# Layer 2 running sums: a written order on TensorE, head-sized state products, and the second norm on ScalarE

## The chip, the cores and the metric

The kernel runs on one core of a Trainium2 chip. The metric is device microseconds of one launch, taken as the median of several runs. Besides the timed runs there is one execution recorded by the hardware profiler; all durations of single instructions come from it. Engines are named as the profile names them: PE is TensorE's matrix array, PEld its weight load, DVE is VectorE, ACT is ScalarE, POOL is GpSimd, SP is SyncE.

## The reference, cut to what matters

The network has four layers on 4096 tokens of 256 channels (32 tiles of 128 tokens). The change lies in layer 2, a gated linear attention with 8 heads of 32 channels followed by a mixture of experts. Its attention is

```
q, k, v = linear(x)                        # per head 32 channels
k = l2_normalize(k); v = l2_normalize(v)
Z = v (x) k * kv_norm_scale                # one 32x32 matrix per token and head
gates = square(relu(Z . wg + wg_b)) + EPS
Z_scan = cumsum(gates * Z); g_scan = cumsum(gates)
w = exp(sim - running max) / (running sum + EPS)
ctxt = q . (Z_scan / (g_scan + EPS)) * (1 + silu(w))
out = linear(ctxt, wo_w, wo_b)
```

and after `x + out`, the expert layer normalises its input (mean and variance over the 256 channels), adds the normalised rows to the residual, and routes each token to the best two of eight experts by the normalised row:

```
n = layernorm(x); logits = n @ router; top-2; x = x + n + (experts' outputs)
```

The sum `Z_scan` over tokens is what the function `attn2_sum` computes, in chunks: inside a tile of 128 tokens by a 128x128 table of scores with a triangular mask, from earlier tiles by a 32x32 state per head that is added up tile by tile.

## The kernel before, in words

`run` goes through the layers one after another. Layer 2 is `attn2` (line 1169). It projects all tokens to q, k and v, normalises and gates them, then works out in `attn2_fac` one factor per token and head, and then calls `attn2_sum` (line 1423), the stage that the change rewrites. After it come a short `tile_table` and the experts of layer 2, which start by loading the rows that the last router step scattered to memory.

`attn2_sum` has 16 turns of its loop, one for each pair `u` of token tiles. In a pair:

- POOL multiplies q by the factor (line 1434) and adds the output bias to the residual `t` (1435).
- PE turns q to channels (four transposes, 1439, into the PSUM bank with the tag "o"); ACT copies the result to `qT` (1441).
- PE makes the scores, 16 products of 32 rows by 128 columns (1449), in two PSUM tiles `s`; DVE multiplies each with the triangle to `sm` (1452, 1024 columns, two a pair).
- For each of the two tiles, PE adds into the context bank `c` what earlier tiles give: `before[:, m, :]`, a 128x128 matrix for four heads at once, in which all blocks but the four on the diagonal have to be zero (1462). Then it makes the tile's own state, a 128x128 product of v and k (through the helper at line 146, tile `st_ps`); DVE adds it to the running `state` (1471) and multiplies the sum with a block mask `ones_bd` to make the next `before` (1473). Then PE adds to `c` what the tile itself gives, eight products with 32 output rows (1477).
- ACT scales `c` to `cT` (1484, two a pair); PE multiplies with the output weights (line 146, tile `o_ps`, the same bank "o"); DVE adds this to `t` (1488).

Matrix products are float32; in the profile each stands as two rows, a transpose as one.

In the same loop runs the router step `route` (line 1731) of the four tiles that were finished two pairs before. It is a generator: `next(steps)` runs it to its next `yield`. Its parts are the norm (DVE at line 213, then POOL adds the normalised rows to `t`, line 1741); two sets of four transposes (1747) with a copy on ACT and one on DVE; the router product with 8 columns (through 146, `f_r_ps<-w_r`) and the choice of the best two, some twenty DVE instructions of 0.2 us and an exponential on ACT; a product for the positions, and eight scattering transfers on POOL (1784). The square root of the norm (204) and the exponential (1724) each need their own function table in ACT, so both load one, eight times each.

All these PSUM tiles but `s` have one buffer: "o" (shared by the transposes of q and the output product), "c", "state" and the router's "r". The order of the work on each engine is set by a scheduler that merges the instructions by its own estimate of times; each engine then works its list strictly in order. Nothing in the stage is written by hand. The projection before it does write the order on PE by hand, with `manual_schedule(engines={PE})`: PE's instructions then stand as the program writes them, and the other engines' are still placed by the scheduler.

Of the kernel before, what the change touches and what calls it, by code (L numbers as in the profile page):

```python
# [10 lines left out]
F32 = mybir.dt.float32  # L11
# [77 lines left out]
class Net:  # L89
# [102 lines left out]
    def layer_norm(self, pool, x, out, eps, on_act=False):  # L192
# [16 lines left out]
        for i in range(n):  # L209
            if on_act:  # L210
                nc.scalar.activation(to(i), x[:, i, :], AF.Identity, bias=shift[:, i : i + 1], scale=r[:, i : i + 1])
            else:
                nc.vector.tensor_scalar(to(i), x[:, i, :], mv[:, i, 0:1], r[:, i : i + 1], ALU.subtract, ALU.mult)

# [962 lines left out]
    def attn2(self, t, S):  # L1177

        nc, tc = self.nc, self.tc
        with tc.tile_pool(name="a2", bufs=1) as pool:  # L1180
# [8 lines left out]
            ones_bd = pool.tile([P, 2, P], F32, tag="ones_bd", name="ones_bd")  # L1189
            self.kv_blocks(pool, None, wg_bd)  # L1190
            nc.gpsimd.memset(ones_bd, 0.0)
            for h in range(4):
                hp = slice(h * D, (h + 1) * D)
                nc.gpsimd.memset(ones_bd[hp, :, hp], 1.0)
# [28 lines left out]
            with (  # L1223
# [11 lines left out]
                self.attn2_sum(t, A, ked, ones_bd, wp, ps, route)  # L1235
# [187 lines left out]
    def attn2_sum(self, t, A, ked, ones_bd, wp, ps, route):  # L1423
# [3 lines left out]
        state = wp.tile([P, 2, P], F32, tag="state", name="a2_state", bufs=1)  # L1427
        before = None
        steps = None
        for u in range(NT // 2):  # L1430
            two = slice(2 * u, 2 * u + 2)
            q, k = A["qk"][:, two, 0:C], A["qk"][:, two, C:]
            qh = q.rearrange("p t (h d) -> p t h d", d=D)
            nc.gpsimd.tensor_tensor(qh, qh, bc(A["fac"][:, :, u, :], 3, D), ALU.mult)
            nc.gpsimd.tensor_tensor(t[:, two, :], t[:, two, :], bc(self.row("wo_b"), 1, 2), ALU.add)
            p = ps.tile([P, 2, 2, P], F32, tag="o", name="a2_qT_ps")
            for m in range(2):
                for j in range(2):
                    nc.tensor.transpose(p[:, m, j, :], q[:, j, m * P : (m + 1) * P], self.ident)
            qT = wp.tile([P, 2, 2, P], F32, tag="qT", name="a2_qT")  # L1440
            nc.scalar.copy(qT, p)
            sms = []
            for pair in range(2):
                s = ps.tile([P, 2, 2, 2, P], F32, tag="s", name="a2_s", bufs=2)
                for m in range(2):
                    for j in range(2):
                        for i in range(2):
                            hp = slice((2 * pair + i) * D, (2 * pair + i + 1) * D)
                            nc.tensor.matmul(s[:, i, m, j, :], A["vT"][hp, m, (2 * u + j) * P : (2 * u + j + 1) * P], qT[hp, m, j, :],
# [3 lines left out]
                sms.append(sm.rearrange("p i (m j) n -> p i m j n", m=2))  # L1453
            if steps:
                next(steps, None)
            c = ps.tile([P, 2, 2, P], F32, tag="c", name="a2_c_ps")
            first = True
            for j in range(2):
                ti = 2 * u + j
                for m in range(2):  # L1460
                    if before is not None:
                        nc.tensor.matmul(c[:, m, j, :], before[:, m, :], qT[:, m, j, :], start=first, stop=False)
                        first = False
                if ti < NT - 1:
                    sp = ps.tile([P, 2, P], F32, tag="state", name="a2_st_ps")
                    for m in range(2):
                        self.mm(sp[:, m, :], [(A["v"][:, ti, m * P : (m + 1) * P], k[:, j, m * P : (m + 1) * P])])
                    if ti == 0:
                        nc.vector.tensor_copy(state, sp)
                    else:  # L1470
                        nc.vector.tensor_add(state, state, sp)
                    nxt = wp.tile([P, 2, P], F32, tag="before", name="a2_before", bufs=3)
                    nc.vector.tensor_mul(nxt, state, ones_bd)
                for m in range(2):
                    for h in range(4):
                        hp = slice(h * D, (h + 1) * D)
                        nc.tensor.matmul(c[hp, m, j, :], k[:, j, m * P + h * D : m * P + (h + 1) * D], sms[h // 2][:, h % 2, m, j, :],
                                         start=(before is None and m == 0), stop=(j == 1 and m == 1))
                if before is None:
                    first = False  # L1480
# [985 lines left out]
```

## Time and profile before

| | us |
|---|---|
| median of 3 runs (lowest, highest) | 3781.54 (3780.37, 3785.58) |
| the profiled execution | 3747.99 |
| its span | 3746.2 |
| PE busy in the span | 3401.1 |
| first product of the stage to the end of its last output product | 1795.5 to 2014.2 |
| of this, pairs 0 to 3 (first transposes of q to the end of the scores of pair 4) | 1796.8 to 1852.9 |
| of this, the rest of pair 4 to pair 15 | 1852.9 to 2014.2 |
| end of the last output product to the experts' first load | 2014.2 to 2045.1 |

The profiled execution is some 34 us shorter than the timed runs. Times of day are microseconds from the start of the span. A busy PE is not a PE at its peak: its clock is granted in full or in part, and the profile gives the granted share for any stretch.

### The profile page before, as it was taken

How to read it: one execution, taken by the hardware profiler on the slowest of the kernel's cores; microseconds unless marked ns; L12 is line 12 of the kernel's file. 1: busy time of each engine (PE TensorE's matmuls, PEld its weight loads, DVE VectorE, ACT ScalarE, POOL GpSimd, SP SyncE). 2: the span in 40 equal slices, each digit the busy share in tenths (PEclk: the TensorE clock that was granted, in tenths of full speed). 3: DMA queues.
4: the chain of work that ended last, by engine and by line, in shares of the span. 5: the costliest groups of instructions: out<-in, count | busy, mean ns of one | idle time of the engine just before them, and what ended most of it. 6: DMA issues, size and time to landing. Idle time of an engine off the chain costs nothing. (4 is left out here: it accounts for less than half of the span.)

```text
span 3746.2 us, 59679 instructions
## 1 busy us (share of the span) xinstructions
PE 3401.1 (91%) x22332; PEld 2387.8 (64%) x22332; DVE 2211.1 (59%) x5433; ACT 1360.4 (36%) x2783; POOL 1433.0 (38%) x1416
## 2 busy tenths in 40 slices
PE   6989999999997788887787977999999996999997
PEld 4433333333343688855565755888888885888886
DVE  6756656666565477778665557777777775111111
ACT  5544343443432566433121334222222222323231
POOL 1038888888884455534343433000000001111110
PEclk9999999999998899999786989999999997999999
DMA  1004414401013322200012865223223322555554
GB/s 57 3 28 115 132 42 119 121 24 41 21 41 105 104 68 77 73 19 1 12 44 100 255 219 225 90 96 95 91 91 102 96 91 96 203 191 190 195 186 182
DMA packets 160975, 378.27 MB, mean 101 GB/s; under 512 B 17377, under 2 KB 75490, under 8 KB 151458
## 3 DMA queue, kind: packets, MB, share of 16 engines
q1 hardware_dynamic: 136450, 318.96, 26.2%
q0 software_dynamic: 13056, 35.93, 2.5%
q10 hardware_dynamic: 11168, 19.42, 1.5%
q8 instruction: 182, 2.98, 0.3%
q14 instruction: 119, 0.97, 0.1%
HBM read 273.96 MB, written 100.29 MB: 100 GB/s over the span
## 5 line engine op out<-in xcount | busy, mean ns | idle before, releaser
L583 POOL TENSOR_TENSOR l_sm<-l_sc,mask 128x512 f32<-128x512 f32 (+3 forms) x624 | 770.0, 1271 | 118.6 <-ACT l_sc L573 116.2
L577 DVE TENSOR_TENSOR l_sm<-l_s,mask 128x256 f32<-128x256 f32 (+3 forms) x1248 | 492.6, 448 | 299.9 <-PE l_s L567 290.3
L573 ACT COPY l_sc<-l_s 128x384 f32<-128x384 f32 (+3 forms) x896 | 367.8, 461 | 556.9 <-PE l_s L567 540.9
L567 PE MATMUL l_s<-l_q,l_k 32*128 32x384 f32 (+2 forms) x3584 | 423.6, 513 | 7.4 <-ACT l_sc L573 4.1
L1784 POOL DMA_INDIRECT xs<-f_n,f_to x64 | 62.8, 981 | 788.0 <-DVE a_qt L2096 576.5
L146 PE MATMUL f_h_ps<-f_xT,f_w 128*128 128x256 f32 x1440 | 346.5, 389 | 13.9 <-ACT f_h L1898 5.8
L1925 POOL DMA_INDIRECT ys<-f_y,f_at x144 | 138.8, 964 | 575.4 <-ACT f_y L1924 527.3
L146 PE MATMUL f_y_ps<-f_w,f_h 128*128 128x256 f32 x1440 | 328.1, 379 | 0.0
L146 PEld LDWEIGHTS f_h_ps<-f_xT,f_w 128*128 128x128 f32 x1440 | 266.2, 192 | 83.1 <-ACT f_h L1898 31.6
L567 PEld LDWEIGHTS l_s<-l_q,l_k 32*128 32x128 f32 x3584 | 164.9, 183 | 240.5 <-issue 123.2
L146 PEld LDWEIGHTS f_y_ps<-f_w,f_h 128*128 128x128 f32 x1440 | 268.2, 190 | 33.6
L2144 ACT ACTIVATE a_e<-a_e 128x512 f32<-128x512 f32 x256 | 156.9, 629 | 241.3 <-DVE a_e L2117 240.4
L952 DVE TENSOR_TENSOR l_pr<-l_vk,l_w_ps 128x1280 f32<-128x1280 f32 x128 | 186.6, 1482 | 55.1 <-PE l_acc_ps L956 37.7
L1898 ACT ACTIVATE f_h<-f_h_ps,f_w 128x256 f32<-128x256 f32 x360 | 163.6, 468 | 134.3 <-PE f_h_ps L146 134.2
L956 PE MATMUL l_acc_ps<-ident,l_pr 128*128 128x128 f32 x1600 | 196.9, 277 | 9.4 <-POOL l_pr L947 9.2
L956 PEld LDWEIGHTS l_acc_ps<-ident,l_pr 128*128 128x128 f32 x1600 | 183.5, 143 | 15.7 <-POOL l_pr L947 10.9
L1924 ACT ACTIVATE f_y<-f_y,f_wgt 128x256 f32<-128x256 f32 x144 | 65.3, 500 | 328.6 <-DVE f_y L1922 295.8
L610 PE MATMUL l_a_ps<-l_sm,l_v 128*32 128x512 f32 (+3 forms) x1408 | 178.2, 528 | 2.6 <-POOL l_sm L583 2.5
L610 PE MATMUL l_b_ps<-l_sm,l_v 128*32 128x256 f32 (+2 forms) x2176 | 171.5, 376 | 0.5 <-POOL l_sm L583 0.5
L2128 PE MATMUL a_sa_ps<-a_q,a_kt 128*128 128x256 f32 x512 | 155.2, 385 | 17.9 <-DMA a_kt<-a_kd 9.3
L2132 ACT COPY a_u<-a_sa_ps 128x256 f32<-128x256 f32 x128 | 47.6, 372 | 328.3 <-PE a_sa_ps L2128 328.3
L1922 DVE TENSOR_TENSOR f_y<-f_y_ps,f_w 128x512 f32<-128x512 f32 x72 | 49.8, 691 | 196.7 <-PE f_y_ps L146 190.4
(500 smaller groups left out, 6301.1 us busy)
## 6 DMA issues: line engine op xcount, KB each, us to landing
a_kt<-a_kd SPq DMA_DIRECT2D x128, 512.0 KB
f_w<-in_f_w SPq DMA_DIRECT2D x36, 1152.0 KB
f_w<-in_f_w SPq DMA_DIRECT2D x36, 1028.0 KB
xs<-zero SPq DMA_DIRECT2D x8, 4160.0 KB
l_vk<-vt SPq DMA_DIRECT2D x180, 128.0 KB
f_x<-xs SPq DMA_DIRECT2D x72, 260.0 KB
f_w<-in_f_w SPq DMA_DIRECT2D x36, 384.0 KB
l_rcp<-l_recd SPq DMA_DIRECT2D x48, 256.0 KB
```

The costliest lines, as they stand in the source:

```text
L146: self.nc.tensor.matmul(out, lhsT, rhs, start=(i == 0), stop=(i == len(pairs) - 1))
L567: nc.tensor.matmul(s[pair, j], k[hp, key * P : (key + 1) * P], qs[hp], start=True, stop=True)
L573: nc.scalar.copy(sc[:, j], s[1, j])
L577: nc.vector.tensor_tensor(sms[0][:, j, at : at + t * wide].rearrange("p (t n) -> p t n", n=wide), part[:, which, :], mask, ALU.mult)
L583: nc.gpsimd.tensor_tensor(sms[1][:, :, at : at + t * wide].rearrange("p j (t n) -> p j t n", n=wide), part[:, :, which, :], bc(mask, 1, 2) ...
L610: nc.tensor.matmul(out, v[:, key, hp], sms[pair][:, j, base + lo * wide : base + hi * wide], start=not seen[nm], stop=(left[nm] == 0 and h ...
L952: nc.vector.tensor_tensor(pr, vk, bc(held["w"][:, j, dy], 3, D), ALU.mult)
L956: nc.tensor.matmul(acc[:, m, j, :], pf[:, dx, m * P : (m + 1) * P], self.ident, is_transpose=True, start=(j == 0 and dy == 0 and dx == 0 a ...
L1898: nc.scalar.activation(h[:, m, :], q, AF.Gelu, bias=w1[:, 2 * hidden + m : 2 * hidden + m + 1])
L1925: nc.gpsimd.indirect_dma_start(out=self.ys_parts[(i % 4) * NI + k], in_=y[:, k, :], in_offset=None, out_offset=bass.IndirectOffsetOnAxis(a ...
L2128: mm = lambda out, i, right: nc.tensor.matmul(out, A[i], right, start=True, stop=True)
L2144: nc.scalar.activation(e[:, i : i + 3 : 2], e[:, i : i + 3 : 2], AF.Exp, scale=1.0 / 16.0)
```

## The change

- PE's order in the stage is written out. A turn of the loop issues: the transposes of q of the next pair (`turn`), the states of this pair (`states`), the output product of the pair before (`out`), one step of the router, the context of this pair (`context`), the scores of the next pair (`scores`), and another step of the router.
- What earlier tiles give is applied head by head: four 32x32 products for each half of the channels (`earlier`) in place of one 128x128 product. The off-diagonal blocks of the state are thus never read, and the mask `ones_bd` with its multiplication goes. `before[ti+1]` is itself the running sum (a DVE add from `before[ti]` and PSUM).
- The states of both tiles of a pair are made together, in one PSUM bank.
- `earlier` for both tiles stands in front of `within`, what the tiles themselves give.
- The router's norm of layer 2 is made on ACT (`on_act`, line 211: scale and shift), and so is the sum of the residual and the normalised rows: `t*(r+1)+shift`, four ACT instructions in place of one on POOL. DVE makes the shift and `r+1`, two small instructions.

```diff
+        return r, (shift if on_act else None)
...
-            ones_bd = pool.tile([P, 2, P], F32, tag="ones_bd", name="ones_bd")
...
-            nc.gpsimd.memset(ones_bd, 0.0)
-            for h in range(4):
-                hp = slice(h * D, (h + 1) * D)
-                nc.gpsimd.memset(ones_bd[hp, :, hp], 1.0)
...
-                self.attn2_sum(t, A, ked, ones_bd, wp, ps, route)
+                self.attn2_sum(t, A, ked, wp, ps, route)
...
-    def attn2_sum(self, t, A, ked, ones_bd, wp, ps, route):
+    def attn2_sum(self, t, A, ked, wp, ps, route):
         nc, w = self.nc, self.w
         tri = self.triangle(wp)
...
+        qTs, sms, before, cTs = {}, {}, {}, {}
+        two = lambda u: slice(2 * u, 2 * u + 2)
+        keys = lambda ti: A["qk"][:, ti, C:]
+        def scale(u):
+            qh = A["qk"][:, two(u), 0:C].rearrange("p t (h d) -> p t h d", d=D)
             nc.gpsimd.tensor_tensor(qh, qh, bc(A["fac"][:, :, u, :], 3, D), ALU.mult)
...
+            nc.gpsimd.tensor_tensor(t[:, two(u), :], t[:, two(u), :], bc(self.row("wo_b"), 1, 2), ALU.add)
+        def turn(u):
             p = ps.tile([P, 2, 2, P], F32, tag="o", name="a2_qT_ps")
             for m in range(2):
                 for j in range(2):
...
+                    nc.tensor.transpose(p[:, m, j, :], A["qk"][:, 2 * u + j, m * P : (m + 1) * P], self.ident)
+            qTs[u] = wp.tile([P, 2, 2, P], F32, tag="qT", name="a2_qT")
+            nc.scalar.copy(qTs[u], p)
+        def scores(u):
+            sms[u] = []
             for pair in range(2):
                 s = ps.tile([P, 2, 2, 2, P], F32, tag="s", name="a2_s", bufs=2)
                 for m in range(2):
                     for j in range(2):
                         for i in range(2):
                             hp = slice((2 * pair + i) * D, (2 * pair + i + 1) * D)
...
+                            nc.tensor.matmul(s[:, i, m, j, :], A["vT"][hp, m, (2 * u + j) * P : (2 * u + j + 1) * P], qTs[u][hp, m, j, :],
                                              start=True, stop=True)
                 sm = wp.tile([P, 2, 4, P], F32, tag="sm", name="a2_sm", bufs=3)
                 nc.vector.tensor_tensor(sm, s.rearrange("p i m j n -> p i (m j) n"), bc(bc(tri, 1, 4), 1, 2), ALU.mult)
...
+                sms[u].append(sm.rearrange("p i (m j) n -> p i m j n", m=2))
+        def states(u):
+            sp = ps.tile([P, 2, 2, P], F32, tag="state", name="a2_st_ps")
+            for j in range(2):
+                for m in range(2):
+                    self.mm(sp[:, j, m, :], [(A["v"][:, 2 * u + j, m * P : (m + 1) * P], keys(2 * u + j)[:, m * P : (m + 1) * P])])
             for j in range(2):
                 ti = 2 * u + j
...
+                before[ti + 1] = wp.tile([P, 2, P], F32, tag="before", name="a2_before", bufs=4)
+                if ti == 0:
+                    nc.vector.tensor_copy(before[1], sp[:, 0])
+                elif ti < NT - 1:
+                    nc.vector.tensor_add(before[ti + 1], before[ti], sp[:, j])
+        def context(u):
+            c = ps.tile([P, 2, 2, P], F32, tag="c", name="a2_c_ps")
+            def earlier(j, first):
                 for m in range(2):
                     for h in range(4):
                         hp = slice(h * D, (h + 1) * D)
...
+                        nc.tensor.matmul(c[hp, m, j, :], before[2 * u + j][hp, m, hp], qTs[u][hp, m, j, :], start=(first and m == 0), stop=False)
+            def within(j, first):
+                for m in range(2):
+                    for h in range(4):
+                        hp = slice(h * D, (h + 1) * D)
+                        nc.tensor.matmul(c[hp, m, j, :], keys(2 * u + j)[:, m * P + h * D : m * P + (h + 1) * D], sms[u][h // 2][:, h % 2, m, j, :],
+                                         start=(first and m == 0), stop=(j == 1 and m == 1))
+            if u == 0:
+                within(0, True)
+                earlier(1, False)
+            else:
+                earlier(0, True)
+                earlier(1, False)
+                within(0, False)
+            within(1, False)
+            cTs[u] = wp.tile([P, 2, 2, P], F32, tag="cT", name="a2_cT")
             for m in range(2):
...
+                nc.scalar.activation(cTs[u][:, m], c[:, m], AF.Identity, scale=ked[:, m, 0:1])
+        def out(u):
             o = ps.tile([P, 2, C], F32, tag="o", name="a2_o_ps")
             for j in range(2):
...
+                self.mm(o[:, j, :], [(cTs[u][:, kt, j, :], w["w_o2"][:, kt, :]) for kt in range(2)])
+            nc.vector.tensor_add(t[:, two(u), :], t[:, two(u), :], o)
+        U = NT // 2
+        steps = []
+        def step():
+            for s in list(steps):
+                if next(s, self) is self:
+                    steps.remove(s)
+        with self.tc.manual_schedule(engines={mybir.EngineType.PE}):
+            scale(0)
+            scale(1)
+            turn(0)
+            scores(0)
+            for u in range(U + 1):
+                if u + 2 < U:
+                    scale(u + 2)
+                if u + 1 < U:
+                    turn(u + 1)
+                if u < U:
+                    states(u)
+                if u > 0:
+                    out(u - 1)
+                step()
+                if u > 0 and u % 2 == 0:
+                    steps.append(route(2 * u - 4, TPB))
+                if u < U:
+                    context(u)
+                if u + 1 < U:
+                    scores(u + 1)
+                step()
+            while steps:
+                step()
     def attn2_any(self, t):
-        self.layer_norm(wp, t[:, tiles, :], n[:, :, :C], 1e-5)
+        r, shift = self.layer_norm(wp, t[:, tiles, :], n[:, :, :C], 1e-5, on_act=(L == 2))
...
-            nc.gpsimd.tensor_tensor(t[:, tiles, :], t[:, tiles, :], n[:, :, :C], ALU.add)
+            nc.vector.tensor_scalar_add(r, r, 1.0)
+            for i in range(T):
+                nc.scalar.activation(t[:, t0 + i, :], t[:, t0 + i, :], AF.Identity, bias=shift[:, i : i + 1], scale=r[:, i : i + 1])
```

Of the rewritten function the lines removed are left out here; they are those of the function printed above.

## The prediction

> **What bounds the kernel now.** I read the page first, for the shape of the whole:
>
> ```profile
> span 3746.2 us, 59679 instructions
> PE 3401.1 (91%) x22332; PEld 2387.8 (64%) x22332; DVE 2211.1 (59%) x5433; ACT 1360.4 (36%) x2783; POOL 1433.0 (38%) x1416
> PEclk9999999999998899999786989999999997999999
> ```
>
> PE is busy 91% of the span, but its clock drops to 7 and 8 tenths around slices 20 to 23; the stage that the change rewrites lies there (1795 to 2045 us). Next the busy time by stretches: pairs 0 to 3, the other pairs, what follows the last output product, and one period of two pairs.
>
> ```profile
> core 0: us, PE busy (x) PEld busy (x) DVE busy (x) ACT busy (x) POOL busy (x), PEclk, DMA share, GB/s
> 1796.80:1852.90 56.10, 49.26 (x441) 38.95 (x441) 32.34 (x85) 11.22 (x20) 22.37 (x22) 0.79 0.02 8
> 1852.90:2014.20 161.30, 141.89 (x1218) 112.42 (x1216) 100.34 (x322) 35.72 (x63) 60.05 (x59) 0.80 0.11 39
> 2014.20:2045.10 30.90, 13.19 (x47) 10.92 (x46) 16.37 (x74) 3.56 (x5) 16.57 (x16) 0.50 0.30 99
> 1877.60:1905.00 27.40, 24.15 (x213) 19.41 (x213) 17.04 (x57) 6.30 (x11) 10.38 (x11) 0.81 0.11 40
> ```
>
> No engine is full: DVE has 17.0 of 27.4 us, ACT 6.3. PE is busy 24.2, at 0.81 of the clock: it loses time twice, by 3.2 us of idling a period and by running half of it slowly. Then the same period in windows of 3.41 us:
>
> ```profile
> 1882.07:1885.48 3.41, 2.29 (x27) 1.45 (x31) 3.15 (x7) 0.00 (x0) 2.50 (x4) 1.00 0.22 79
> 1888.89:1892.31 3.42, 3.42 (x33) 3.13 (x33) 2.04 (x7) 0.58 (x1) 0.19 (x1) 1.00 0.02 5
> 1892.31:1895.72 3.41, 3.41 (x36) 3.08 (x32) 3.17 (x16) 1.49 (x2) 0.00 (x0) 0.50 0.00 0
> 1895.72:1899.13 3.41, 3.18 (x23) 2.12 (x22) 2.52 (x11) 0.00 (x0) 0.00 (x0) 0.50 0.00 0
> 1899.13:1902.55 3.42, 3.42 (x26) 2.69 (x26) 1.51 (x7) 0.84 (x2) 0.00 (x0) 0.50 0.00 0
> 1902.55:1905.96 3.41, 2.63 (x15) 2.05 (x14) 2.04 (x9) 0.26 (x1) 1.97 (x2) 1.00 0.11 39
> ```
>
> The clock changes only on this grid (it falls at 1865.0, 1892.3, 1919.6, 1946.9, 1974.2, each time for three windows). The window before the fall is the one with the router product of 8 columns. The timeline gives prices and waits:
>
> ```profile
> 1879.00 1.72 PE L1449 MATMUL a_s<-a_qT,a_vT 32*128 32x128 f32 x32 [0.73 <-ACT a_qT L1441]
> 1882.38 0.41 PE L1477 MATMUL a_c_ps<-a_sm,a_qk 128*32 128x128 f32 x4 [1.02 <-DVE a_sm L1452]
> 1884.20 0.63 PE L1477 MATMUL a_c_ps<-a_sm,a_qk 128*32 128x128 f32 x12 [0.80 <-DVE a_sm L1452]
> 1884.76 0.71 PE L1462 MATMUL a_c_ps<-a_qT,a_before 128*128 128x128 f32 x4
> 1885.40 0.65 PE L1477 MATMUL a_c_ps<-a_sm,a_qk 128*32 128x128 f32 x16
> 1888.53 0.60 PE L1747 MATMUL f_r_ps<-ident,a_qk 128*128 128x128 f32 x4
> ```
>
> PE stands before the scores until ACT has copied qT, and before the context until DVE has masked them.
>
> **The change, part by part**
>
> *PE's work.* Prices at full clock, from one start to the next: scores (32 rows) 1.65 us; 4 rows of 128x128 0.65; 16 rows of 128x32 0.57; output product (1886.70 to 1888.32) 1.62; transposes of q 0.54; the router's two sets of transposes 0.55 each; router product (1890.07 to 1891.95) 1.88; the two products for the positions 0.7 together (0.64 each at half clock, 1896.42).
>
> *The 32x32 products.* A pair gets 32 rows of them for 8 rows of 128x128 (1.30 us). No 32x32 row is in the trace. Neighbours: 0.57/16 = 0.036 us a row with 32 output rows, 1.65/32 = 0.052 with 32 input rows, 0.16 if no two of them overlap. So 1.14, 1.65 or 5.1 us a pair. I take 0.036: the weights are 32 columns wide, as in the 128x32 rows. The ends give +8 us and +62 us over 15.5 pairs. The Trainium skill's page "TensorEngine Tiling (Array Packing)", Gotcha 1 in "Restrictions and Gotchas", speaks against this edit: row tiles may not use one PSUM bank at the same time, and all four heads write bank `c`; no run here shows that yet, and by it each row would take its 0.16 and the sum below would end at 3807.
>
> A pair now costs 0.54 + 1.30 + 1.62 + 1.14 + 1.14 (within) + 1.65 = 7.4 us of PE, two pairs with the router 14.8 + 1.1 + 1.88 + 0.7 = 18.5 us, against the 27.3 us that two take.
>
> *DVE.* The mask goes (31 x 0.42 us) and the norm (32 x 0.42); the shift and r+1 come (16 x 0.17). That is worth nothing alone, since DVE is 62% busy, but brings `before` sooner. *POOL.* The sum goes (8 x 2.38 us); only the scatters stand behind it, whose eight issues (8 x 1.28 = 10.2 us) fit in a period. The mask's memsets were hidden in the stage before. SP issues nothing in the stage; the loads of layer 3's weights wait, as now, for the last output product. *ACT* gets 64 instructions of about 0.52 us (four in a row took 2.08 us in the projection): 4.2 us in a period, to 6.3.
>
> *The written order, and what waits in it.* I go through a period, counted from the end of the router product, at full clock. PE: context 0 to 2.3, scores to 3.9. DVE, once it has the logits: choice of the two best 2.9 us (2025.54 to 2028.46), with the norm's statistics of the next router step among them 1.2 us: the choice is ready at 4.2, its running sums at 5.1. PE's two position products wait for these: done at 5.5 (0.9 us idle). Transposes of q to 6.0, states to 7.3. Meanwhile ACT, in order: table and root (1.48) to 3.5, table and exponential (1.48) to 5.0, two cT (0.84) to 5.9, four norm instructions (2.08) to 8.0, and only then the copy of qT, to 8.6. The output product uses the bank that this copy frees: it starts at 8.7 (1.4 us idle). Behind that copy on ACT stand the sum into `t`, four instructions that also need r+1 from DVE (9.2), and the first copy of the router's transposes, to 11.9; the second set of transposes, at 15.0, is the next to need that bank. The second pair runs without a wait, since masked scores (DVE, 8.2), `before` (9.7) and cT are in time. Idle 2.3 us, so a period is 18.5 + 2.3, with handovers 20.9 us (0.1 taken for them).
>
> *The clock.* Counting columns times the share of the array in use, without transposes, the windows before a fall hold 930 at most; the least that kept the clock holds 1090 (1882.07). At half clock 1340 stayed down and 1410 rose. The 32x32 rows count 1/16, so a window with router product and `earlier` holds 680 to 1100 by its phase. I estimate a fall in half of the six periods, two windows each, 1.7 us lost in each window: 10 us. Ends: none, 0; three windows in every period as now, 31 us. The page "TensorE: Matmul & The Clock Gate" (Part 1) would have the clock fall after an idle window only; the trace contradicts it (busy 3.42 of 3.42 us before the fall). By the rule there would be no fall, and the sum 10 us less.
>
> *Sum.* Pairs 0 to 3: the first two at half clock (pair 0: 1.2 us wait for qT, 2.8 scores, 0.75 + 2.3 + 3.0 + 2.8 + 0.75 = 13.6; pair 1: 0.75 + 2.3 + 3.1 + 2.3 + 1.65 = 10.1), then 7.7 and 8.8: 40 us for 56, gain 16 (19 if the clock rises at 1807 as now). Pairs 4 to 15: 6 x 20.9, less the missing transposes and scores of a pair 16 (2.2), plus the last cT and output product (2.7), plus 10 for the clock: 136 us for 161, gain 25. The tail: the last router steps now come after the last output product. Router product at half clock 3.5, choice 4.2, positions 1.0, then two sets of transposes with their copies 5, the last router product 3.6, its choice 2.9, positions and places 1.3. So the last eight scatters start 21.5 us after the output product, now 17.2 (2031.44): loss 4.3. Together 37 us.
>
> The profiled execution had 3747.99 us (span 3746.2) and the timed runs a median of 3781.54, 0.9% more; I take the difference from the one off the other: 3781.5 - 37 = 3745. 0.2% (7.5 us) is about what a measurement of this kernel can tell from no change.
>
> **The rivals**
>
> 1. *The 32x32 rows take turns.* Four row tiles into one bank; the existing scores split neighbouring heads over two banks. Against it: the four write different partitions. At 0.16 us a row, 3807 us: slower. It decides from 37/15.5 = 2.4 us a pair, 0.11 us a row.
> 2. *The clock falls in each period as now.* For it: the router product stays, and the 32x32 rows fill less of the array. Then 31 us are lost for 10, with the gain of the start at 16: 3766.
> 3. *In-order waits take the place of the old ones.* The copy of qT and the position products stand behind DVE and ACT chains; POOL did part of ACT's work. If ACT's norm came one position earlier than its shift, PE would wait through it: nothing is gained once waits reach 27.3 - 18.5 = 8.8 us a period, for the 2.3 I count. At 6 us: 3767; at 9: 3785.
> 4. *The change does less than it says*, because PE had slack anyway: against it, PE is busy 24.2 of 27.4 us and nothing else is.
>
> **How the numbers follow.** Forecast 0.56 (3727 to 3757: no fall and an early rise 3730, 32x32 rows at 0.052 us 3753); rival 2 0.20; rival 3 0.13 (half of it faster, a third within, the rest slower); rival 1 0.10; 0.01 for the fourth. Faster: 0.56 + 0.20 + 0.065 = 0.83; within 0.2%: 0.05; slower: 0.12. The range has to reach rivals 2 and half of 3: 3725 to 3772. The forecast's own is 3727 to 3757.
>
> **What would show it.** In the profile after: the stage from the first transposes to the last output product takes about 176 us for 217; a period is 21 to 25 us; the 32x32 rows 0.04 us each, start to start; PE waits for the running sums before the position products and for the copy of qT before the output product, and hardly for masked scores; half clock in one or two windows of some periods; 31 us from the last output product to the first expert load become 35. Wrong would make it: 32x32 rows of 0.1 us or more; three slow windows in each period; a wait of over 4 us in front of the output product; or later stages that do not simply start earlier.

## The result, and the profile after

| | kernel before | changed kernel |
|---|---|---|
| median of 4 runs each (us) | 3782.67 | 3749.53 |
| lowest, highest (us) | 3780.37, 3785.58 | 3749.39, 3752.91 |
| ratio, 95% interval | | 0.9914 (0.9897 to 0.9931) |

The change takes 33 us off; 3745 was forecast, in a range of 3725 to 3772. (Of all runs below, one of the kernel before on the third chip took 4066.83 us at a lower granted clock and is counted in no figure.) The profiles don't show those 33 us. The page of the changed kernel (span, PE's busy time, granted clock in 40 slices):

```profile
span 3747.9 us, 60403 instructions
PE 3391.5 (90%) x22708; PEld 2386.9 (64%) x22708; DVE 2183.0 (58%) x5386; ACT 1389.2 (37%) x2845; POOL 1412.2 (38%) x1403
PEclk9999999999998899999886989999999997999998
```

Its profiled execution (3749.59 us) agrees with its timed runs, while that of the kernel before (3747.99 us) was 34 us shorter than its own. So the spans differ by 1.7 us, in the wrong direction, and the clock still drops in slices 20 to 22. The same stretches as before, in the changed kernel: pairs 0 to 3, the other pairs, the time from the last output product to the experts' first load, and one period of two pairs.

```profile
core 0: us, PE busy (x) PEld busy (x) DVE busy (x) ACT busy (x) POOL busy (x), PEclk, DMA share, GB/s
1799.05:1831.56 32.51, 31.39 (x480) 26.73 (x480) 18.50 (x36) 12.24 (x24) 15.35 (x17) 0.90 0.01 2
1831.56:2003.98 172.42, 142.89 (x1547) 117.77 (x1545) 83.63 (x300) 59.06 (x112) 47.53 (x54) 0.82 0.11 38
2003.98:2039.55 35.57, 15.76 (x59) 13.60 (x59) 18.51 (x99) 7.80 (x14) 15.58 (x16) 0.50 0.28 90
1866.64:1895.28 28.64, 23.15 (x261) 19.63 (x260) 14.04 (x50) 10.10 (x19) 7.88 (x9) 0.82 0.11 39
```

The first pairs are better than forecast (32.5 us for 40; 56.1 before) and the tail is as forecast (35.6 for 35). But pairs 4 to 15 take 172 us, more than before (161), and a period is 28.6 us where I had worked out 20.9 and the kernel before has 27.4. PE idles 5.5 us in it. The timeline of PE's weight loads in that period says for what, and POOL's shows what runs meanwhile:

```profile
1875.47 0.81 PEld L1477 LDWEIGHTS a_c_ps<-a_qT,a_before 32*32 32x32 f32 x32 [0.17 <-issue]
1876.48 0.78 PEld L1483 LDWEIGHTS a_c_ps<-a_sm,a_qk 128*32 128x32 f32 x20 [0.20 <-issue]
1877.86 0.17 PEld L1483 LDWEIGHTS a_c_ps<-a_sm,a_qk 128*32 128x32 f32 x6 [0.60 <-issue]
1878.62 0.16 PEld L1483 LDWEIGHTS a_c_ps<-a_sm,a_qk 128*32 128x32 f32 x4 [0.59 <-issue]
...
1880.38 0.66 PEld L1450 LDWEIGHTS a_s<-a_qT,a_vT 32*128 32x128 f32 x4 [0.20 <-issue]
1881.53 0.52 PEld L1450 LDWEIGHTS a_s<-a_qT,a_vT 32*128 32x128 f32 x4 [0.49 <-issue]
1882.98 0.52 PEld L1450 LDWEIGHTS a_s<-a_qT,a_vT 32*128 32x128 f32 x4 [0.93 <-issue]
...
1887.28 1.37 PEld L1450 LDWEIGHTS a_s<-a_qT,a_vT 32*128 32x128 f32 x12 [0.42 <-issue]
```

```profile
1875.77 0.98 POOL L1826 DMA_INDIRECT xs<-a_qk,f_to  x1 [7.02 <-ACT t L1783]
...
1884.63 0.96 POOL L1826 DMA_INDIRECT xs<-a_qk,f_to  x1 [0.30 <-issue]
```

The 32 rows of 32x32 take 1.0 us, and then, from 1877 to 1887 us, while POOL issues its eight scatters, the next rows come in groups of one to six, most of them about 0.72 us or twice that apart, with idle time put down to "issue": PE waits for nothing that the profile shows. Counted in the full list of these loads, 32 rows come between 1877.86 and 1887.28; undisturbed, the same kind takes 1.0 to 1.65 us. I call this starving: PE stands although nothing that the profile shows holds it. That it has no instruction to run is one reading and is not shown; the trace has no transfer of instructions under way between 1873.1 and 1888.5 us, so at least no slow one fills the gaps. The windows of 3.41 us, laid on the grid on which the clock changes, show what goes with it:

```profile
1874.08:1877.50 3.42, 3.34 (x60) 2.51 (x59) 2.48 (x10) 2.54 (x5) 1.43 (x2) 1.00 0.05 19
1877.50:1880.91 3.41, 1.68 (x16) 0.94 (x16) 0.00 (x0) 0.00 (x0) 2.50 (x4) 1.00 0.27 98
1880.91:1884.32 3.41, 1.93 (x9) 1.44 (x10) 0.00 (x0) 0.00 (x0) 2.80 (x3) 0.50 0.32 117
1884.32:1887.74 3.42, 1.87 (x12) 1.75 (x13) 0.19 (x1) 0.35 (x1) 0.96 (x2) 0.50 0.21 78
1887.74:1891.15 3.41, 3.41 (x23) 3.19 (x22) 2.86 (x3) 0.76 (x3) 0.00 (x0) 0.50 0.02 5
```

PE is busy half of the time, DVE and ACT wait for it, and the clock falls at 1880.9 for three windows. The same happens in each of the five periods between 1853 and 1980 us, once for four windows. The profile of the kernel before has scatters beside PE as well (1876 to 1886 us) without such gaps. So two things were open: why the two executions of the kernel before differ by 34 us, and what starves PE in the changed kernel.

### The profile page after: what moved, and what is told of

It is laid out like the page before. It is cut to its first block, busy times and chain, and to the rows that moved or that the text cites. A ratio compares the mean times of both kernels' runs of the same rounds, so it can differ in the third digit from the quotient of the medians.

```text
span 3747.9 us, 60403 instructions
## 1 busy us (share of the span) xinstructions
PE 3391.5 (90%) x22708; PEld 2386.9 (64%) x22708; DVE 2183.0 (58%) x5386; ACT 1389.2 (37%) x2845; POOL 1412.2 (38%) x1403
## 3 DMA queue, kind: packets, MB, share of 16 engines
q8 instruction: 185, 3.03, 0.3%
## 5 line engine op out<-in xcount | busy, mean ns | idle before, releaser
L953 DVE TENSOR_TENSOR l_pr<-l_vk,l_w_ps 128x1280 f32<-128x1280 f32 x128 | 186.5, 1481 | 55.8 <-PE l_acc_ps L957 37.7
```

Of the source, the lines that this page charges most:

```text
L953: nc.vector.tensor_tensor(pr, vk, bc(held["w"][:, j, dy], 3, D), ALU.mult)
```

## The experiments

The experiments ran on three chips, each beside the kernel before on the same chip; which chip the runs of the first table had is not on record. "Stage" is the first transposes of q to the end of the last output product in the profiled execution, "period" the time between the ends of router products in its middle.

| run | median us | ratio to the kernel before beside it (95%) | stage us | period us |
|---|---|---|---|---|
| first chip, before 3751.60 us (19 runs) | | | | |
| e1 before, unchanged | 3754.63 | 1.0004 (0.9994 to 1.0013) | 215.8 | 27.4 |
| e2 changed, same work and order | 3680.78 | 0.9808 (0.9792 to 0.9825) | 141.1 | 17.9 |
| e3 before, same work and order | 3751.56 | 1.0001 (0.9990 to 1.0012) | 216.6 | 27.4 |
| e4 changed, 128x128 product and mask | 3690.30 | 0.9832 (0.9815 to 0.9848) | 147.4 | 18.0, 19.6 |
| second chip, before 3775.88 us (15 runs) | | | | |
| e5 changed, unchanged | 3739.27 | 0.9906 (0.9886 to 0.9926) | 198.2 | 27.4 to 29.5 |
| e6 changed, norm on DVE | 3735.87 | 0.9895 (0.9878 to 0.9911) | 194.8 | 19.6, 35.2 |
| e7 changed, scatters held | 3765.22 | 0.9973 (0.9961 to 0.9986) | 140.9 | 17.9 |
| e8 before, 32x32 products alone | 3779.27 | 1.0002 (0.9988 to 1.0015) | 248.6 | 31.2 to 33.9 |
| third chip, before 3778.02 us (13 runs) | | | | |
| e9 as e7, with plain stores in the loop | 3768.52 | 0.9972 (0.9961 to 0.9982) | 140.5 | 17.9 |
| e10 order and state bank alone | 3757.22 | 0.9941 (0.9917 to 0.9964) | 211.1 | 28.8 to 30.7 |
| e11 changed, unchanged | 3745.75 | 0.9913 (0.9891 to 0.9935) | 203.6 | 28.3 to 30.1 |
| e12 as e6 | 3737.57 | 0.9887 (0.9859 to 0.9915) | 208.0 | 19.7 to 35.4 |

**e1, the kernel before, unchanged.** No edit.

> The kernel before, unchanged. It settles which of its two times, 3748 us (the profiled execution) or 3782 us (the median of its timed runs), the gain is to be counted from. Theory A, the gain of 33 us lies in the stage as the prediction has it: the runs take 3780 to 3786 us, and a new profile that is as long shows the stage (first transposes to last output product) at about 240 us in place of 217.4. Theory B, the 34 us are spent elsewhere in the timed runs: a profile of 3780 us has the stage at 217 us again and later stages longer. If it takes 3748 us throughout, the change is worth nothing and the 33 us belong to how the kernel before was started.

It took 3754.63 us (3748.01 to 3758.56), its profile has a span of 3749.6 us and a stage of 215.8. None of the three theories holds as put; the third had the time, but not what follows from it (e2 is 71 us faster here). On this chip the short time is the time of all the runs, and the 3782 us belong to the conditions of the first timed runs.

**e2, scatters collected for after the loop.**

```diff
-        for i in range(T):
-            for r in range(2):
-                nc.gpsimd.indirect_dma_start(...)
+        def scatter():
+            for i in range(T):
+                for r in range(2):
+                    nc.gpsimd.indirect_dma_start(...)
+        S["late"].append(scatter)      # layer 2; called after attn2_sum
...
                 self.attn2_sum(t, A, ked, wp, ps, route)
+                for scatter in S.pop("late"):
+                    scatter()
```

> The changed kernel with the 64 scattering transfers of the router held back until the loop is over; nothing is left out. In the profile of the changed kernel each period of two pairs takes 28.6 to 30.2 us, and PE stands for its own instructions in bursts while POOL issues the eight scatters. Theory A, the scatters starve PE: without them in the loop a period takes 19 to 22 us, the stage from the first transposes to the last output product falls from 205 to 150 to 165 us. The 56 scatters more behind the loop cost 56 x 1.27 = 71 us, so the time is 3749.5 + 71 - 45 = 3775 us (3765 to 3790). Theory B, PE starves by its own rate of instructions, whatever the scatters do: the periods stay at 28 to 30 us and the time is 3749.5 + 71 = 3820 us (3812 to 3825).

The edit did nothing: POOL's order is not written by hand, and the scheduler put the scatters back where their places are known. Each engine holds the same instructions in the same order as in the changed kernel. So e2 tests neither theory. It is the changed kernel again, and on this chip it took 3680.78 us, 71 less than the kernel before beside it. The stretches of its windows that answer to those above, and a period in its timeline on PE:

```profile
1797.20:1830.41 33.21, 32.09 (x481) 27.27 (x481) 18.51 (x36) 12.25 (x24) 15.36 (x17) 0.87 0.01 2
1830.41:1938.30 107.89, 103.70 (x1541) 91.69 (x1539) 82.76 (x300) 59.00 (x112) 42.83 (x49) 1.00 0.15 54
1938.30:1974.38 36.08, 15.68 (x67) 13.50 (x65) 18.63 (x99) 7.80 (x14) 20.42 (x21) 0.55 0.33 111
1872.23:1890.11 17.88, 17.23 (x268) 15.27 (x264) 13.85 (x51) 10.10 (x19) 7.91 (x10) 1.00 0.17 61
```

```profile
1872.07 1.07 PE L1480 MATMUL a_c_ps<-a_qT,a_before 32*32 32x128 f32 x32
1873.07 1.08 PE L1486 MATMUL a_c_ps<-a_sm,a_qk 128*32 128x128 f32 x32
1874.08 1.72 PE L1453 MATMUL a_s<-a_qT,a_vT 32*128 32x128 f32 x32
1875.73 0.41 PE L146 MATMUL f_r_ps<-f_both,before 128*128 128x32 f32 x2
...
1876.83 1.06 PE L146 MATMUL a_st_ps<-a_qk,a_v 128*128 128x128 f32 x8
1878.53 1.99 PE L146 MATMUL a_o_ps<-w_o,a_cT 128*128 128x256 f32 x8 [0.65 <-ACT a_qT L1443]
...
1888.16 1.85 PE L146 MATMUL f_r_ps<-w_r,a_v 128*128 128x8 f32 x16
```

PE is busy 103.7 of 107.9 us at full clock, the only wait of the period shown is 0.65 us for the copy of qT, and the scatters run all the while (DMA share 0.15). Here they don't starve PE.

**e3, the same edit in the kernel before.**

> The kernel before with its 64 scatters held back until the loop is over; nothing is left out. Theory A, the 34 us by which its timed runs exceed its profiled execution are PE starving under the scatters: 3782 + 71 - 34 = 3819 us (3808 to 3825), with the stage at 210 to 217 us. Theory B, those 34 us have nothing to do with the scatters: 3782 + 71 = 3853 us (3845 to 3860). Against e2 this gives what the change is worth where no scatter runs beside it: by the terms of the prediction 37 to 50 us.

For the same reason no edit in effect, and no difference: 3751.56 us. The 34 us are not settled by it.

**e4, the 32x32 products undone.**

```diff
-                    for h in range(4):
-                        hp = slice(h * D, (h + 1) * D)
-                        nc.tensor.matmul(c[hp, m, j, :], before[2 * u + j][hp, m, hp], qTs[u][hp, m, j, :], ...)
+                    nc.tensor.matmul(c[:, m, j, :], before[2 * u + j][:, m, :], qTs[u][:, m, j, :], ...)
...
-                    nc.vector.tensor_add(before[ti + 1], before[ti], sp[:, j])
+                    nc.vector.tensor_add(state, state, sp[:, j])
+                if ti < NT - 1:
+                    nc.vector.tensor_mul(before[ti + 1], state, ones_bd)
```

> The changed kernel with one part undone: what earlier tiles give is again one 128x128 product for each half of the channels, with the mask and its multiplication on DVE; order, states and norm stay as changed. By the prediction's rows the 32x32 products are worth 0.16 us a pair on PE, or 0.3 us by the rows measured after (1.00 us for 1.30), and the clock is lost a little more by the smaller share of the array: 3749.5 + 3 to 5 us, so 3750 to 3757 us. Rival, the 24 rows more in a pair (48 instructions) feed the starving of PE: without them 16 x 48 = 768 instructions fall away, and the time falls by 5 to 20 us, to 3730 to 3745 us.

Both numbers were set against the wrong base. Beside e2, on the same chip, it is 9.5 us slower; 6.3 of them lie in the stage. Its periods are 18.0 and 19.6 us in turn. In both kinds DVE, which has the mask back, is late with the running sums (1.06 us, in place of the 0.65 for qT); in the long ones the clock also falls for one window (windows and timeline of e4):

```profile
1876.44:1879.85 3.41, 2.35 (x38) 2.12 (x35) 3.31 (x17) 3.37 (x8) 0.00 (x0) 1.00 0.00 0
1879.85:1883.26 3.41, 3.41 (x14) 3.05 (x13) 2.65 (x10) 1.64 (x4) 0.00 (x0) 0.50 0.00 0
```

```profile
1879.00 0.41 PE L146 MATMUL f_r_ps<-f_cum,all_one 128*128 128x32 f32 x2 [1.06 <-DVE f_cum L1818]
```

So the written order, with the common state bank and ACT's norm, carries some 61 of the 71 us, and the 32x32 products add 9.5. PE's rows take the same time (1.00 us, and 0.98 to 1.07 for the 128x128 rows), so the 6.3 us in the stage come by way of DVE and the clock; where the other 3.2 us lie is open.

**e5, the changed kernel again.** No edit.

> The changed kernel, unchanged. e2 turned out to hold the same instructions in the same order on every engine as the changed kernel (its scatters were placed early again), and yet took 3681 us with periods of 17.9 us, where the changed kernel's profile has 3748 us with periods of 28.6 to 30.2 us. Theory A, the starving of PE belongs to the chip or to where the program was loaded, not to the kernel: then the changed kernel also takes 3675 to 3690 us when e2's conditions hold again, 60 to 75 us less than the kernel before beside it, with periods of 17 to 19 us; under the first conditions it takes 3749 us again and the kernel before 3782 us. Theory B, a detail of e2 that the order does not show (the place of a wait, the line of an instruction in its block) took the starving away: 3749 us beside a kernel before of about 3752 us.

Theory A: on this chip the kernel before takes 3775.88 us, the changed one 3739.27, and its profile shows the broken rows again; both times are 7 to 10 us below those of the first table. Same instructions as e2, 58 us more, 57 of them in the stage.

**e6, the norm back on DVE, the sum on POOL.**

```diff
-        r, shift = self.layer_norm(..., 1e-5, on_act=(L == 2))
+        r, shift = self.layer_norm(..., 1e-5)
-            nc.vector.tensor_scalar_add(r, r, 1.0)
-            for i in range(T):
-                nc.scalar.activation(t[:, t0 + i, :], t[:, t0 + i, :], AF.Identity, bias=..., scale=...)
+            nc.gpsimd.tensor_tensor(t[:, tiles, :], t[:, tiles, :], n[:, :, :C], ALU.add)
```

> The changed kernel with one part undone: the norm of the router is again made on DVE and the sum on POOL (the shift, r+1 and eight ACT instructions a step go). By the prediction ACT's norm costs PE 1.4 us a period before the output product, since the copy of qT stands behind it, against DVE's 1.7 us a step: undoing it should gain 0.6 us (the wait measured after) to 1.4 us in six periods, 4 to 8 us, if DVE and POOL have the room; POOL's sum of 2.4 us stands before or between the scatters, which end the tail, so 1 to 3 us may be lost there. Theory A: 2 to 8 us below the changed kernel in e5. Rival, the norm on DVE delays masked scores and the choice: 5 to 15 us above e5.

3.4 us below e5, as theory A has it, but the intervals overlap. Its timeline shows something else. Its scatters fall at other places of the period, and the loss shows at other places too. Here the eight issues run from 1881.03 to 1890.95:

```profile
1883.01 0.97 PEld L146 LDWEIGHTS a_st_ps<-a_qk,a_v 128*128 128x128 f32 x8
1885.97 1.59 PEld L146 LDWEIGHTS a_o_ps<-w_o,a_cT 128*128 128x128 f32 x8 [2.00 <-issue]
1887.59 1.97 PEld L146 LDWEIGHTS f_r_ps<-w_r,a_v 128*128 128x128 f32 x16
1889.58 0.36 PEld L1477 LDWEIGHTS a_c_ps<-a_qT,a_before 32*32 32x32 f32 x15
1890.99 0.17 PEld L1477 LDWEIGHTS a_c_ps<-a_qT,a_before 32*32 32x32 f32 x4 [1.04 <-issue]
1892.43 0.64 PEld L1477 LDWEIGHTS a_c_ps<-a_qT,a_before 32*32 32x32 f32 x13 [1.27 <-issue]
1893.45 1.48 PEld L1483 LDWEIGHTS a_c_ps<-a_sm,a_qk 128*32 128x32 f32 x32 [0.38 <-issue]
1895.32 2.81 PEld L1450 LDWEIGHTS a_s<-a_qT,a_vT 32*128 32x128 f32 x32 [0.38 <-issue]
```

Output and router products, whose rows take 0.12 to 0.2 us, pay one gap of 2 us and then run at their usual 1.6 and 2.0 us; the first 32x32 rows behind them, at 0.03 us each, break up at once. The period that ends with this router product took 19.6 us; those with the next scatters beside context and scores took 34.2 to 35.3. But the short period passes its loss on: the clock falls at 1891.13 for four windows, and rows without a scatter beside them then take twice their time (1.48 us for 0.81, 2.81 for 1.53). A short and a long period together take 54.8 us, two of e5's 57.6. So these scatters are not shown to be cheaper than those beside context and scores.

**e7, the scatters held in truth.** Over e2, the offsets are read from a copy that exists only when all places are known:

```diff
+                held = wp.tile([P, 2, NT], I32, tag="held", name="f_held", bufs=1)
+                nc.vector.tensor_copy(held, S["to"])
                 for scatter in S.pop("late"):
-                    scatter()
+                    scatter(held)
```

> The changed kernel with the 64 scatters really held until all places are known: their offsets are read from a copy that DVE makes after the last router step. Nothing is left out. The 56 scatters more behind the loop cost 56 x 1.27 = 71 us. Theory A, a scatter costs PE nothing but where PE starves: if e5 takes 3681 us, this one takes 3681 + 71 = 3752 us (3742 to 3758) with periods of 17 to 19 us; if e5 starves (3749 us), this one still has periods of 17 to 20 us, and takes 3745 to 3765 us. Theory B, the starving has nothing to do with scatters: beside an e5 of 3749 us this takes 3815 to 3825 us with periods of 28 to 30 us.

Theory A, its time 0.2 us above the range put. On the chip on which e5 starves, the loop without scatters runs as e2 does (windows of e7: the stage, one period):

```profile
1799.13:1940.05 140.92, 135.61 (x2019) 118.83 (x2019) 101.23 (x335) 71.25 (x136) 16.52 (x23) 0.97 0.01 2
1873.90:1891.80 17.90, 17.26 (x264) 15.29 (x268) 13.85 (x51) 10.11 (x19) 0.19 (x1) 1.00 0.01 2
```

The stage is 57 us shorter than in e5. Behind it the 64 scatters stand alone from 1962 to 2043 us, 1.27 us each, so the whole is 26 us slower than e5. In e5 six of the eight batches, 48 scatters, run inside the stage: beside PE a scatter cost 57/48 = 1.2 us, alone 1.27.

**e8, the 32x32 products alone, in the kernel before.**

```diff
-                    if before is not None:
-                        nc.tensor.matmul(c[:, m, j, :], before[:, m, :], qT[:, m, j, :], start=first, stop=False)
+                    for h in range(4):
+                        hp = slice(h * D, (h + 1) * D)
+                        if before is not None:
+                            nc.tensor.matmul(c[hp, m, j, :], before[hp, m, hp], qT[hp, m, j, :], start=(j == 0 and m == 0), stop=False)
...
-                    nc.vector.tensor_mul(nxt, state, ones_bd)
+                    nc.vector.tensor_add(nxt, before, sp)
```

> The kernel before with one part of the change alone: the states applied by four 32x32 products without mask, in the order that the scheduler gives. The product is 0.3 us a pair cheaper (1.00 for 1.30 us) and the mask (31 x 0.42 us) leaves DVE, but PE's order and its waits stay. Theory A, the order carries the gain (e4, without the 32x32 products, had 61 us of it): this one takes 0 to 10 us less than the kernel before. Rival, the mask on DVE's chain from state to the next product is what PE waits for: 15 to 40 us less.

No difference (1.0002, 0.9988 to 1.0015): the low end of theory A. In the scheduler's order the cheaper product and the missing mask don't reach the end. Its profile is the nearest that there is to the kernel before on a starving chip: stage 248.6 us, 33 more than e1, periods of 31 to 34 us for 27.4. The loss has another form here. Rows break up in one of its periods alone; in most the rows run whole and DVE is released late (timeline of e8, PE's weight loads and DVE):

```profile
1883.45 1.53 PEld L1448 LDWEIGHTS a_s<-a_qT,a_vT 32*128 32x128 f32 x32 [0.97 <-issue]
1890.74 1.23 DVE L1451 TENSOR_TENSOR a_sm<-a_s,tri 128x1024 f32<-128x1024 f32 x1 [3.29 <-remote]
1892.02 0.61 PEld L1475 LDWEIGHTS a_c_ps<-a_sm,a_qk 128*32 128x32 f32 x12 [3.98 <-DVE a_sm L1451]
```

"Remote" stands where no instruction that the profile knows ends near the signal. The scores end at 1885.2 by their rows, yet PE's signal for them comes at 1890.7, just after POOL's batch of scatters (1879.5 to 1889.4). The second masking (DVE) thus starts 5.8 us after the last load of its scores, in e1 2.5 us. Such signals, 1 us and more behind the last row that gives one, stand by each of the six batches in the stage of this profile and of the changed kernel's (e5 and e11 too). In the stages of the kernel before, e1, e2, e4, e7 and e9 there is none over 0.5 us. A PE that has started its rows and doesn't finish them would show this as well as one that lacks instructions.

**e9, as e7, with other traffic beside PE.**

```diff
+            for i in range(T):
+                for r in range(2):
+                    row = (2 * (t0 + i) + r) * P
+                    nc.sync.dma_start(out=self.xs_copy[row : row + P, :], in_=n[:, i, :])
```

> e7 (scatters held until the loop is over) with work added: in the loop, where the eight scatters of a router step stood, SP issues eight plain stores of the same rows to a memory of their own, 128 rows of 1040 bytes each. It asks whether PE starves under any such traffic or under POOL's scatters alone. Where PE starves (kernel before at 3770 us or more): Theory A, the traffic to memory is enough: periods of 24 to 30 us in place of e7's 17.9, and 40 to 60 us above e7's 3765. Theory B, it takes POOL's indirect transfers: periods of 17.5 to 19 us, 3755 to 3775 us. Where the kernel before takes about 3752 us this tells nothing of it, and both theories give 17.9 us and 3750 to 3760 us.

Theory B. On this chip e11 starves, and yet beside the stores PE runs on (windows and timeline of e9 at one batch of stores):

```profile
1882.00:1884.00 2.00, 2.00 (x19) 1.63 (x21) 1.71 (x8) 1.13 (x3) 0.00 (x0) 1.00 0.81 273
1884.00:1886.00 2.00, 2.00 (x66) 1.60 (x60) 1.15 (x5) 1.45 (x4) 0.00 (x0) 1.00 0.67 225
```

```profile
1883.82 0.81 PEld L1482 LDWEIGHTS a_c_ps<-a_qT,a_before 32*32 32x32 f32 x32 [0.17 <-issue]
1884.82 0.81 PEld L1488 LDWEIGHTS a_c_ps<-a_sm,a_qk 128*32 128x32 f32 x32 [0.20 <-issue]
1885.84 1.53 PEld L1455 LDWEIGHTS a_s<-a_qT,a_vT 32*128 32x128 f32 x32 [0.20 <-issue]
```

The stores move 225 to 273 GB/s, twice the 117 of the scatters in the starved windows above, and the same rows are whole. So it is not traffic to memory as such. Which property of the scatters does it is not shown: that POOL issues them, where they write, or that a batch lasts 10 us where the stores take some 4.

**e10, order and state bank alone** (the edits of e4 and e6 together).

> The changed kernel with two parts undone: the 128x128 product with its mask is back, and the norm is on DVE with the sum on POOL. What is left is the written order on PE and both states in one bank. Theory A, these alone carry the gain: where PE does not starve 3684 to 3700 us (e4 had 3690 with ACT's norm), 52 to 68 us below the kernel before beside it; where it starves 25 to 40 us below it. Rival, mask and norm together fill DVE (31 x 0.42 and 32 x 0.42 us come back) until PE waits for the choice and the masked scores: periods of 21 us or more without starving, and 20 to 40 us above e11.

Neither as put. By the medians it is 21 us below the kernel before and 11.5 above e11, and it starves too. Between 1830 and 2000 us its list of waits has PE waiting 8.3 us for qT before the output product and 6.2 us for the running sums. The second wait is in e4 as well (6.6 us in the same stretch), where nothing starves, so it belongs to the mask and not to the broken rows.

**e11, the changed kernel a third time.** No edit.

> The changed kernel, unchanged, as the measure for the other three. Theory A, which of its times comes goes with the kernel before beside it: 3675 to 3690 us beside one of 3745 to 3755 us, 3737 to 3752 us beside one of 3770 to 3785 us. Rival, its starving goes with each loading of the program by itself: any other pair, 3681 beside 3780 or 3745 beside 3750.

Theory A: 3745.75 beside 3778.02. On each of the three chips all profiled kernels agree: on one, none starved; on two, each with scatters in the loop did, by broken rows, late signals or both. The kernel before itself was not profiled on those two.

**e12, e6 again.**

> The changed kernel with the norm on DVE and the sum on POOL, as in e6, where it stood 3.4 us below the changed kernel, with intervals that overlap. Theory A, ACT's norm costs PE its wait before the output product: 2 to 8 us below e11, most plainly where PE does not starve. Rival, it makes no difference: within 2 us of e11.

8.2 us below e11 by the medians, with a spread of 22 us of its own (3730.33 to 3752.08). On both chips the norm on DVE is the lower, in neither by more than the intervals. Of the versions run it is the fastest on the starving chips; that it beats the changed kernel is not shown.

## Why the prediction was right, point by point

The total was right by luck: errors of about the same size cancel. Where PE doesn't starve, the gain is 3751.6 - 3680.8 = 71 us, about twice the 37 I forecast. In the first runs the changed kernel took 3749.5 - 3680.8 = 69 us more than that and the kernel before 3782.7 - 3751.6 = 31 us more, and 71 - 69 + 31 = 33 is what was measured. This sum is bookkeeping between chips. That the scatters beside PE make most of the 69 is shown on one chip (e5 against e7, 57 us in the stage); that they make the 31 is not.

By the signs it named, the prediction's picture of the stage was wrong in the profile of the changed kernel: the stage took 203.6 us for 176, a period 28.6 for 21 to 25, the clock stood at half for three or four windows in every period, and once PE stood 4.3 us in front of an output product. Two of these it had listed as what would make it wrong.

- **The base.** "I take the difference from the one off the other" was the weak step. The 34 us between the profiled execution and the timed runs of the kernel before were not a constant that both kernels share: the e1 runs on the first chip have the profile's time. All my prices came from an execution without starving, and the timed base was very likely one with it. That the kernel before lost its 31 us in this stage is likely from e8 (33 us there), but no profile of it on such a chip exists, and it was not run there with its scatters held.
- **32x32 rows.** Taken at 0.036 us, measured 1.00 us for 32, 0.031 each. Rival 1 is out, and so is, for this use, Gotcha 1 of the Trainium skill's page "TensorEngine Tiling (Array Packing)" ("Restrictions and Gotchas"): four row tiles write one PSUM bank here without taking turns, where 0.16 us a row would have shown it.
- **The period.** Forecast 20.9, measured 17.9 in e2 (six of them: 18 us). The order of events was right and three sizes were off: PE's work was 17.2 us for 18.5 (states 0.89 us for 1.30, context 2.0 for 2.3), the choice and running sums came in time before the position products (0.9 us foreseen, none measured), and the wait for qT was 0.65 us in the period shown (3.8 us in five waits between 1830 and 1940) for 1.4.
- **The clock.** I gave 10 us; in e2 the granted clock is 1.00 from 1830 to 1938 us, nothing lost. My count of columns times the share of the array was the wrong measure. In e4 it fell after a window in which PE waited (busy 2.35 of 3.41 us), in the changed kernel after windows of 1.35 to 2.17 us; but other windows of e4 with 2.35 us kept it, and one of the changed kernel with 2.15. The kernel before, where it fell after a window that was busy throughout, remains an exception to any rule by idle time, and no exact condition is shown. Rival 2 is out for e2, where no window from pair 4 to pair 15 is slow. In the profile of the changed kernel its three slow windows a period did come, but behind windows in which PE starved (1.68 of 3.41 us busy) and not behind the router product. Rival 4 is out as well: PE's busy time in the stage is 135.8 us in e2 for 191.2 before.
- **Pairs 0 to 3 and the tail.** 33.2 us in e2 for 40, 36.1 for 35. The first two pairs were priced at half clock, which rose at 1805.5 already. Against e1's 55.8, 160.0 and 30.4 us the three stretches of e2 give 22.6 + 52.1 - 5.7 = 69 us.
- **Rival 3**, a wait in place of those removed, named the right kind of loss and the wrong wait. The waits for DVE and ACT that I counted stayed small. What came is starving: against e2 the period shown is 10.8 us longer, 4.8 us by more idle time (5.5 for 0.65) and 5.9 by a PE that is busy longer (23.2 for 17.2) at a clock of 0.82 for 1.00. It is not a queue order that causes it, since every engine's order is that of e2. That POOL's eight issues "fit in a period" held for POOL and overlooked what the scatters do to PE.

Another sign of being wrong, "later stages that do not simply start earlier", didn't come: from the first expert product to the end e2 takes 1701.3 us, e1 1702.9.

## What to carry to other kernels

A profile and a median that differ by 0.9% are two measurements under different conditions: find out which one the prices hold for before subtracting a difference from either. Wherever indirect transfers run beside a tight instruction stream, look at PE's idle time "<-issue" and at waits for PE put down to "remote". Here the faster kernel lost the more (58 to 69 us, the kernel before some 31). And count a loss over whole rounds of the loop: in e6 the period that looks cheap hands a slow clock to the next.

## What the runs showed of the hardware that was not expected

- On two chips of three, and in the first profile of the changed kernel, PE's short rows start in small groups about 0.72 us apart, or multiples of it, while POOL issues indirect scatters (1.27 us each, 1040 bytes to a row); 32 rows then took 9.4 us in place of 1.0 to 1.65. PE's signals come late as well (in e8 5.5 us behind scores whose rows ran whole). Plain stores of the same rows at 225 to 273 GB/s don't do this on a chip that starves. On the third chip the same program with the same scatters shows none of it.
- Why a chip does or doesn't starve is open. The page counts the same transfers of instructions in both (185 packets, 3.03 MB in that queue, in e2 as in the changed kernel). Whether it is the chip itself, or where the program and the scattered rows came to lie in its memory, can't be told from runs on three chips.
- The cost differs by kernel. The kernel before, with 213 rows in a period of 27 us, took about 31 us more; the changed one, with 268 in 18 us, 58 to 69, both with six batches of scatters in the stage. That the rate of rows decides is a guess: the two differ in their order too.
